# Sums over states after every second unit instead of every fourth, and dt's two matmuls half a unit apart

## The chip, the cores and the metric

One core of one Trainium2 chip runs the whole program in one launch. The time is the device time of one execution in microseconds. The engines are TensorE (PE), VectorE (DVE), ScalarE (ACT), GpSimd (POOL) and SyncE (SP), which issues every DMA here. Each engine takes its own instructions strictly in order; semaphores make one wait for another. PSUM, the memory that PE writes, has eight banks of 128 x 512 float32.

## The reference, cut to what matters

Two layers run one after the other on 8 images of 64 x 64 tokens with 192 channels. The first is a chunked state-space layer with convolutions and an MLP in front of and behind it. In the second, half of the channels go through convolutions and the other half through a selective scan in four directions; that scan is where the change lies:

```python
x_dbl = jnp.einsum('bkdl,kcd->bkcl', xs4, x_proj_w)      # xs4: the four directions, 192 channels
dts, Bs, Cs = ...                                        # 6, 16 and 16 rows of x_dbl
delta = jax.nn.softplus(jnp.einsum('bkrl,kdr->bkdl', dts, dt_proj_w) + dt_proj_b[None, :, :, None])
A = -jnp.exp(A_logs)
def step(h, t):
    u_t, d_t, b_t, c_t = t
    h = jnp.exp(d_t[..., None] * A) * h + (d_t * u_t)[..., None] * b_t[:, :, None, :]
    return (h, jnp.einsum('bkdn,bkn->bkd', h, c_t))      # the sum over the 16 states
```

## The kernel before

**Tiling.** A step is 1024 of an image's 4096 tokens in one pair of directions: 8 steps per image. A step has three tiles of 128 channel rows. A tile has 16 units. A unit is 8 channel rows times 16 states, so 128 partitions by 1024 columns. That gives 384 units per image and 3072 in all. "Place" below is a unit's number in its tile, 0 to 15.

**A unit.** `fetch` (L1432, SP) reads dt from DRAM, repeated for the 16 states, six units ahead. `decay` (L1437, ACT) makes exp(dt A) of it in place, two units at a time. `spread` (L1445, PE) makes dt u for all states by one matmul for each half of the columns, into one of two buffers of two banks each. `weigh` (L1462, DVE) multiplies that with B in place. `scan` (L1469, DVE) runs the recurrence into a tile h. POOL saves the last column as the carry (L1471) and multiplies h with C in place (L1472). `gather` (L1483, PE) sums over the states.

**The sums.** `gather` is called at unit q for the four units q-5 to q-2, in every fourth unit. The constant `k["gather"]` has 32 columns, of which 8 hold something. The four units go to four groups of 32 partitions of one bank, one matmul each, for one half of the columns; half a unit later ACT copies the bank to y (L1488), and the other half of the columns follows in another bank, with its copy another half unit later. Two units on, `store` (L1496) issues four DMAs of 8 x 1024.

**dt.** `prepare` is a generator that makes the next tile's dt and dt u while the current tile's units run. It yields the number of the half unit at which it wants to go on. At the first half of place 0 it issues both dt matmuls (L1390), each into a bank of its own, half a unit later both softplus (L1394, ACT), later the product du = dt u (L1396, POOL), the store of dt (L1399), the split of du into three bf16 terms (L1404 to L1410, ACT and POOL by turns) and their DMAs (L1413, L1421).

**The order.** It is written out by hand; `pin` keeps it. The loop over q issues, for each unit: `fetch`, `weigh`, a new `gather` or `store` where due, and then two halves. Each half goes on with the gather, then with the work beside (`beside.half`), then with `prepare`; the first half ends with `spread(q + 1)` and `scan(q)`, the second, in odd units, with two decays. The work beside is everything else: the layers of the next image and the convolutions, sums and outputs of the one before, as generators that yield a cost at each piece. Each half adds a rate to a credit; the work beside runs until the credit is used up, and `beside.spend` charges the scan's own matmuls to it.

**Banks.** Everything but the spread takes single banks from a ring of four (`cx.one`): dt, the sums and all of the work beside. Who takes a bank waits until the last reader of its former contents is done.

**Buffers.** `np_` is a pool of two buffers for each name unless `bufs` says otherwise: y has two, h seven (`4 + BEHIND + 1` with `BEHIND = 2`).

Of the kernel before, what the change touches and what calls it, by code (L numbers as in the profile page):

```python
# [9 lines left out]
F32 = mybir.dt.float32  # L10
# [28 lines left out]
LC = 1024  # L39
UD = 128 // NS  # L40
UN = 128 // UD
DTS = (64, 96)
# [1257 lines left out]
def selective_scan(cx, us, ys, beside, images, start_image, tail):  # L1300
# [8 lines left out]
    nc, tc, pin, k = cx.nc, cx.tc, cx.pin, cx.k  # L1309
    AHEAD, BEHIND = 6, 2  # L1310
    halves = [slice(q * 512, (q + 1) * 512) for q in range(LC // 512)]
# [10 lines left out]
    def order(ap, g):  # L1322
        return reversed_free(ap) if g == 1 else ap
# [8 lines left out]
    with (  # L1332
# [7 lines left out]
        dAs, dBs, hs, late = {}, {}, {}, []  # L1340
# [36 lines left out]
        def prepare(n):  # L1377

            m, t = tiles[n]
            image, g, s = steps[m]
            rows = rows_of[m][0]
            bias = k["dtb"][:, g, t : t + 1]
            dl, du = (wp.tile([128, LC], F32, tag=v, name=v) for v in ("dl", "du"))
            pss = [cx.one("ps_dt") for here in halves]
            for ps, at, here in zip(pss, DTS, halves):
                took = slice(at, at + 2 * RK)
                pin(nc.tensor.matmul(ps, lhsT=k["dtw"][took, g, t, :], rhs=rows[took, here], start=True, stop=True))  # L1390
            beside.spend(1.2)
            yield 1
            for ps, here in zip(pss, halves):
                pin(nc.scalar.activation(dl[:, here], ps, AF.Softplus, bias=bias))  # L1394
            yield 3
            pin(nc.gpsimd.tensor_mul(du, dl, u_of[m][t]))  # L1396
            yield 6
            dld = dp.tile([128, LC], F32, tag="dld", name="dld")
            pin(nc.sync.dma_start(out=dld, in_=dl))  # L1399
            delta_of[n] = dld  # L1400
            yield 7

            terms = wp.tile([128, 3, LC], BF16, tag="terms", name="terms")
            pin(nc.scalar.copy(terms[:, 0, :], du))  # L1404
            yield 9
            pin(nc.gpsimd.tensor_sub(du, du, terms[:, 0, :]))
            yield 11
            pin(nc.scalar.copy(terms[:, 1, :], du))
            yield 13
            pin(nc.gpsimd.tensor_sub(terms[:, 2, :], du, terms[:, 1, :]))  # L1410
            yield 17
            dud = dp.tile([3, 128, LC], BF16, tag="dud", name="dud")
            pin(nc.sync.dma_start(out=dud.rearrange("s p l -> p s l"), in_=terms))  # L1413
            yield 21

            dus = np_.tile([128, UN // 2, 512], BF16, tag="dus", name="dus")
            for half in range(2):
                for odd in range(2):
                    at = 32 * (2 * odd + half)
                    for v in range(3):  # L1420
                        pin(nc.sync.dma_start(  # L1421
                            out=dus[at + UD * v : at + UD * (v + 1)],
                            in_=dud[v].rearrange("(i odd c) l -> odd c i l", odd=2, c=UD)[odd][:, :, halves[half]],
                        ))
                if half == 0:
                    yield 23
            du_of[n] = dus
# [22 lines left out]
        def of(q):  # L1450

            n, i = units[q]
            m, t = tiles[n]
            image, g, s = steps[m]
            more = s != (L // LC - 1, 0)[g]
            bc = bc_of[m, (i // 8 if t == 2 else t)]
            return *bc, carries[image, g][:, t, i : i + 1], 0 if g == 1 else LC - 1, g, more

        def weigh(q):

            dBs[q] = dBs[q].rearrange("p a b -> p (a b)")
            pin(nc.vector.tensor_mul(dBs[q], dBs[q], of(q)[0]))  # L1462

        def scan(q):

            _, C_, carry, last, g, more = of(q)
            dA, dB = dAs.pop(q), dBs.pop(q)
            h = hs[q] = np_.tile([128, LC], F32, tag="h", name="h", bufs=4 + BEHIND + 1)
            pin(nc.vector.tensor_tensor_scan(order(h, g), order(dA, g), order(dB, g), carry, ALU.mult, ALU.add))  # L1469
            if more:  # L1470
                pin(nc.gpsimd.tensor_copy(carry, h[:, last : last + 1]))  # L1471
            pin(nc.gpsimd.tensor_mul(h, h, C_))  # L1472

        def gather(q):

            n, i = units[q]
            m, t = tiles[n]
            image, g, s = steps[m]
            y = np_.tile([128, LC], F32, tag="y", name="y")
            for here in halves:  # L1480
                ps = cx.one("acc")
                for v in range(4):
                    pin(nc.tensor.matmul(  # L1483
                        ps[32 * v : 32 * (v + 1)], lhsT=k["gather"], rhs=hs[q - 3 + v][:, here], start=True, stop=True
                    ))
                beside.spend(1.6)
                yield
                pin(nc.scalar.copy(y[:, here], ps))  # L1488
            for v in range(4):
                del hs[q - 3 + v]  # L1490
            late.append((ys(image)[g][t][UD * (i - 3) : UD * (i + 1), s * LC : (s + 1) * LC], y))

        def store():
            rows, y = late.pop()
            for v in range(4):
                pin(nc.sync.dma_start(out=rows[UD * v : UD * (v + 1)], in_=y[32 * v : 32 * v + UD]))  # L1496

        for t in range(3):
            load(0, t)
# [4 lines left out]
        for _ in prepare(0):  # L1504
            pass
# [5 lines left out]
        coming, due, following, gathering = None, 0, None, iter(())  # L1511
        for q in range(U + BEHIND):
            n, at = divmod(q, UN)
            if q < U:
                m, t = tiles[n]
# [9 lines left out]
                if t == 2 and m + 1 < len(steps):  # L1525
                    image = steps[m + 1][0]
# [9 lines left out]
                if q + AHEAD < U:  # L1536
                    fetch(q + AHEAD)
                weigh(q)
            if (q - BEHIND) % 4 == 3 and q > BEHIND:
                gathering = gather(q - BEHIND)  # L1540
            if (q - BEHIND) % 4 == 1 and q > BEHIND + 1:
                store()
            if q < U:
                for half in range(2):
                    next(gathering, None)
                    beside.half()
                    if coming is not None and 2 * at + half == due:
                        due = next(coming, 2 * UN)
                    if following is not None and t == 2 and at >= UN - 5:
                        next(following, None)  # L1550
                    if half == 0:
                        if q + 1 < U:
                            spread(q + 1)
                        scan(q)
                    elif q % 2 == 1:
                        for ahead in (q + 2, q + 3):
                            if ahead < U:
                                decay(ahead)
        for _ in gathering:
            pass  # L1560
        store()
        beside.finish()
        tail()
# [155 lines left out]
```

## Time and profile before

| What | us |
|---|---|
| runs | 16338.47, 16344.59, 16351.96 |
| their median | 16344.59 |
| the profiled execution's own time | 16347.41 |
| its span, first to last instruction | 16345.0 |
| mean granted TensorE clock | 0.826 |
| first and last scan begin at | 906.3 and 16096.7 |
| an image in the middle (2728 to 4710; 4711 to 6689) | 1982; 1978 |
| PE, DVE, POOL, ACT busy in the second of these | 1630, 1526, 1365, 1142 |
| the last image (14553 to 16100) | 1547 |

The page has one row for each group of instructions: line, engine, operation, output and inputs, shapes and count, then busy time in us and mean duration in ns, then the engine's idle time just before these instructions and what ended most of it. The views of waits give, for an engine's instruction and the instruction that released it, the sum of the idle time in us, how often it occurred, and the longest. A float32 matmul of the source is two rows of PE. Four matmuls on four groups of the array's columns run at the same time, so a row's mean duration is longer than its share of the busy time.

### The profile page before, as it was taken

Reading aid. Unit: us, or ns where it says so; the run is one execution under the profiler, and the core shown is the slowest. Engines: PE = TensorE matmul, PEld = TensorE weight load, DVE = VectorE, ACT = ScalarE, POOL = GpSimd, SP = SyncE. Lnnn points to the kernel's source line nnn. Section 1 sums busy time; section 2 is a strip of 40 time slices with the busy share of each in tenths; the row PEclk is TensorE's granted clock in tenths of the full one; section 3 lists DMA queues with packets and bytes.
Section 4 is the critical chain, followed back from the end, with each engine's and each line's share of the span. In section 5 each row is a group of like instructions: output and inputs, shape, how many; then the busy total and the mean of one; then the engine's idle time right before and its main releaser. Section 6 shows DMA issues by size and latency. Waiting matters only on the chain. (4 is left out here: it accounts for less than half of the span.)

```text
span 16345.0 us, 208335 instructions
## 1 busy us (share of the span) xinstructions
PE 13293.7 (81%) x69608; PEld 4607.8 (28%) x69608; DVE 12235.6 (75%) x9264; ACT 9072.0 (56%) x13776; POOL 10935.8 (67%) x8070
## 2 busy tenths in 40 slices
PE   8977887789887898778888788887887778878866
PEld 4422322333223322233213332133322333211111
DVE  2168887887778867788677886788867887778894
ACT  3355565555665547655466554664656555654643
POOL 3158766876668766687666865678666776667773
PEclk9987787789787897878978798787988889777776
DMA  3288888788787887878878788887888878788885
GB/s 90 83 208 192 209 204 211 199 202 222 187 218 188 210 216 190 221 185 220 213 194 208 189 216 208 204 207 194 219 200 212 204 202 226 188 228 213 208 214 134
DMA packets 1602566, 3241.15 MB, mean 198 GB/s; under 512 B 390152, under 2 KB 841368, under 8 KB 1601496
## 3 DMA queue, kind: packets, MB, share of 16 engines
q1 hardware_dynamic: 1601496, 3227.83, 78.7%
q8 instruction: 556, 9.11, 0.3%
q14 instruction: 514, 4.21, 0.1%
HBM read 2548.91 MB, written 678.18 MB: 197 GB/s over the span
## 5 line engine op out<-in xcount | busy, mean ns | idle before, releaser
L1472 POOL TENSOR_TENSOR h<-h,bc 128x1024 f32<-128x1024 f32 x3072 | 7238.9, 2357 | 1310.3 <-DVE h L1469 1030.6
L1469 DVE TENSOR_TENSOR_SCAN h<-dA,carry,dB 128x1024 f32<-128x1024 f32 x3072 | 7200.3, 2344 | 581.1 <-ACT dA L1437 253.2
L1462 DVE TENSOR_TENSOR dB<-dB,bc 128x1024 f32<-128x1024 f32 x3072 | 3737.5, 1217 | 1860.1 <-PE dB L1445 1855.4
L1437 ACT ACTIVATE dA<-dA,neg_a 128x1024 f32<-128x1024 f32 x3072 | 3378.0, 1150 | 255.2 <-DMA dA<-dld 237.3
L1483 PE MATMUL acc<-h,gather 128*32 128x512 f32 x12288 | 2235.5, 729 | 289.2 <-POOL h L1472 113.9
L1471 POOL COPY carry<-h 128x1 f32<-128x1 f32 x2304 | 422.5, 183 | 2728.3 <-DVE h L1469 2555.1
L1445 PE MATMUL dB<-dus,spread 24*128 24x512 bf16 x6144 | 1386.8, 439 | 866.9 <-DVE h L1469 799.8
L1488 ACT COPY y<-acc 128x512 f32<-128x512 f32 x1536 | 891.6, 580 | 1811.9 <-issue 1021.1
L886 PE MATMUL ps_c<-p,conv_w 96*96 96x512 f32 x2304 | 1261.3, 673 | 31.3 <-ACT p L906 31.3
L1445 PEld LDWEIGHTS <-spread 24*128 24x128 bf16 x6144 | 308.9, 93 | 3074.6 <-issue 1438.0
L690 PE MATMUL ps_y<-X,M 64*64 64x64 f32 x12288 | 613.7, 274 | 419.9 <-issue 187.4
L339 PE MATMUL ps_cv<-pad,diag 64*64 64x512 f32 x6912 | 847.0, 605 | 15.7 <-ACT y L1488 10.0
L618 ACT ACTIVATE M<-ps_d,ln_dt 128x64 f32<-128x64 f32 x3072 | 671.9, 336 | 292.0 <-PE ps_d L624 217.6
L690 PEld LDWEIGHTS ps_y<-X,M 64*64 64x64 f32 x12288 | 559.9, 184 | 598.8 <-issue 233.3
L1483 PEld LDWEIGHTS acc<-h,gather 128*32 128x32 f32 x12288 | 293.7, 117 | 1227.3 <-issue 555.1
L623 PE MATMUL ps_d<-R,after 128*128 128x384 f32 x1024 | 596.8, 675 | 34.1 <-ACT bc L612 16.1
L612 ACT COPY bc<-ps_t 64x256 f32<-64x256 f32 x256 | 93.7, 366 | 929.8 <-PE ps_t L607 929.5
L886 PEld LDWEIGHTS ps_c<-p,conv_w 96*96 96x96 f32 x2304 | 367.5, 177 | 772.4 <-issue 701.4
L1437 ACT ACT_TABLE_LOAD x445 | 570.9, 1283 | 7.9
L1358 PE MATMUL ps_xp<-u,xp 128*108 128x512 f32 x768 | 467.3, 695 | 97.1 <-DMA u<-u 83.6
L1396 POOL TENSOR_TENSOR du<-dl,u 128x1024 f32<-128x1024 f32 x192 | 452.2, 2355 | 136.6 <-DMA bcd<-rows 82.9
L369 PE MATMUL ps_h<-oa,w1a 128*128 128x256 f32 x1536 | 465.0, 424 | 61.0 <-ACT y L1488 21.0
(245 smaller groups left out, 18086.6 us busy)
## 6 DMA issues: line engine op xcount, KB each, us to landing
dA<-dld SPq DMA_DIRECT2D x3072, 512.0 KB
dud<-terms SPq DMA_DIRECT2D x192, 768.0 KB
dus<-dud SPq DMA_DIRECT2D x2304, 64.0 KB
bc<-bcd SPq DMA_DIRECT2D x256, 512.0 KB
y<-yrows SPq DMA_DIRECT2D x256, 384.0 KB
u<-u SPq DMA_DIRECT2D x192, 512.0 KB
dld<-dl SPq DMA_DIRECT2D x192, 512.0 KB
y<-y SPq DMA_DIRECT2D x3072, 32.0 KB
```

What stands on the lines that cost most here:

```text
L339: pin(nc.tensor.matmul(ps[64 * b : 64 * (b + 1)].rearrange("p (h w) -> p h w", w=WW), lhsT=diag[:, t, :], rhs=pad[64 * i : 64 * (i + 1), b ...
L618: pin(nc.scalar.activation(M[:, d, h, :], ps[:, h * S : (h + 1) * S], AF.Exp, bias=bias))
L623: pin(nc.tensor.matmul(ps, lhsT=k["after"], rhs=flat(R[:, d * NH : (d + 1) * NH, :]), start=True, stop=False))
L690: pin(nc.tensor.matmul(psy[d][here, h * HP : (h + 1) * HP], lhsT=M[here, d, h, :], rhs=X[here, d, h, :], start=True, stop=True,))
L886: pin(nc.tensor.matmul(ps.rearrange("p (h w) -> p h w", w=WW), lhsT=w[:, t, :], rhs=pad[:, dy : dy + RB, dx : dx + WW], start=t == 0, stop ...
L1437: pin(nc.scalar.activation(dAs[q], dAs[q], AF.Exp, scale=k["neg_a"][:, steps[m][1], t, i : i + 1]))
L1445: pin(nc.tensor.matmul(dBs[q][:, half, :], lhsT=k["spread"][at : at + 3 * UD, :], rhs=du_of[n][at : at + 3 * UD, i // 2, :], start=True, s ...
L1462: pin(nc.vector.tensor_mul(dBs[q], dBs[q], of(q)[0]))
L1469: pin(nc.vector.tensor_tensor_scan(order(h, g), order(dA, g), order(dB, g), carry, ALU.mult, ALU.add))
L1472: pin(nc.gpsimd.tensor_mul(h, h, C_))
L1483: pin(nc.tensor.matmul(ps[32 * v : 32 * (v + 1)], lhsT=k["gather"], rhs=hs[q - 3 + v][:, here], start=True, stop=True))
L1488: pin(nc.scalar.copy(y[:, here], ps))
```

## The change

`gather` is called in every second unit, for the two units q-3 and q-2. Both halves of the columns of both units go into one bank: first half to partitions 0 to 63, second half to 64 to 127. One copy moves the bank to y, whose shape is now pair, column: two pairs fill one y. `store` runs at the same place and issues four DMAs as before, one for each half of the columns and each unit of a pair, with rows of 512 instead of 1024 values. h has six buffers instead of seven.

`prepare` issues the first dt matmul in half 0, in half 1 its softplus and the second matmul, in half 2 the second softplus, and goes on with du in half 4 instead of 3. Each of the two is charged 1.0 to the credit, where the pair was charged 1.2.

```diff
-            pss = [cx.one("ps_dt") for here in halves]
-            for ps, at, here in zip(pss, DTS, halves):
+            for later, (at, here) in enumerate(zip(DTS, halves)):
+                ps = cx.one("ps_dt")
                 took = slice(at, at + 2 * RK)
                 pin(nc.tensor.matmul(ps, lhsT=k["dtw"][took, g, t, :], rhs=rows[took, here], start=True, stop=True))
-            beside.spend(1.2)
-            yield 1
-            for ps, here in zip(pss, halves):
+                beside.spend(1.0)
+                yield 1 + later
                 pin(nc.scalar.activation(dl[:, here], ps, AF.Softplus, bias=bias))
-            yield 3
+            yield 4
             pin(nc.gpsimd.tensor_mul(du, dl, u_of[m][t]))
...
-            h = hs[q] = np_.tile([128, LC], F32, tag="h", name="h", bufs=4 + BEHIND + 1)
+            h = hs[q] = np_.tile([128, LC], F32, tag="h", name="h", bufs=2 + BEHIND + 2)
...
-            y = np_.tile([128, LC], F32, tag="y", name="y")
-            for here in halves:
-                ps = cx.one("acc")
-                for v in range(4):
+            pair = i // 2 % 2
+            if pair == 0:
+                y = np_.tile([128, 2, 512], F32, tag="y", name="y")
+                late.append((ys(image)[g][t][UD * (i - 1) : UD * (i + 3), s * LC : (s + 1) * LC], y))
+            y = late[-1][1]
+            ps = cx.one("acc")
+            for half, here in enumerate(halves):
+                for v in range(2):
+                    at = 32 * (2 * half + v)
                     pin(nc.tensor.matmul(
-                        ps[32 * v : 32 * (v + 1)], lhsT=k["gather"], rhs=hs[q - 3 + v][:, here], start=True, stop=True
+                        ps[at : at + 32], lhsT=k["gather"], rhs=hs[q - 1 + v][:, here], start=True, stop=True
                     ))
-                beside.spend(1.6)
-                yield
-                pin(nc.scalar.copy(y[:, here], ps))
-            for v in range(4):
-                del hs[q - 3 + v]
-            late.append((ys(image)[g][t][UD * (i - 3) : UD * (i + 1), s * LC : (s + 1) * LC], y))
+            beside.spend(1.6)
+            yield
+            pin(nc.scalar.copy(y[:, pair, :], ps))
+            for v in range(2):
+                del hs[q - 1 + v]

         def store():
-            rows, y = late.pop()
-            for v in range(4):
-                pin(nc.sync.dma_start(out=rows[UD * v : UD * (v + 1)], in_=y[32 * v : 32 * v + UD]))
+            rows, y = late.pop(0)
+            rows = rows.rearrange("(p v c) l -> v c p l", p=2, v=2)
+            for half, here in enumerate(halves):
+                for v in range(2):
+                    at = 32 * (2 * half + v)
+                    pin(nc.sync.dma_start(out=rows[v][:, :, here], in_=y[at : at + UD]))
...
-            if (q - BEHIND) % 4 == 3 and q > BEHIND:
-                gathering = gather(q - BEHIND)
             if (q - BEHIND) % 4 == 1 and q > BEHIND + 1:
                 store()
+            if (q - BEHIND) % 2 == 1 and q > BEHIND:
+                gathering = gather(q - BEHIND)
```

## The prediction

> **What bounds the kernel now.** I read the page first: its busy times (part 1) and its groups (part 5). Part 4, the chain that ended last, names 1% for its largest entry; the kernel has no single chain that could be followed, so I went on to the waits by engine, then to busy times by stage, then to a piece of timeline.
>
> ```profile
> PE 13293.7 (81%) x69608; PEld 4607.8 (28%) x69608; DVE 12235.6 (75%) x9264; ACT 9072.0 (56%) x13776; POOL 10935.8 (67%) x8070
> ...
> L1469 DVE TENSOR_TENSOR_SCAN h<-dA,carry,dB 128x1024 f32<-128x1024 f32 x3072 | 7200.3, 2344 | 581.1 <-ACT dA L1437 253.2
> L1462 DVE TENSOR_TENSOR dB<-dB,bc 128x1024 f32<-128x1024 f32 x3072 | 3737.5, 1217 | 1860.1 <-PE dB L1445 1855.4
> ...
> L1483 PE MATMUL acc<-h,gather 128*32 128x512 f32 x12288 | 2235.5, 729 | 289.2 <-POOL h L1472 113.9
> ```
>
> A unit needs 2.344 + 1.217 = 3.56 us of DVE, but the 3072 scans, which begin at 906.3 and 16096.7 us, stand (16096.7 - 906.3) / 3071 = 4.95 us apart. No engine is full. The largest single loss on DVE is its wait for dB, the spread matmuls of L1445, which stand in PE's queue behind whatever else PE was given. By stage, in one image:
>
> ```profile
> 4960.00:5560.00 600.00, 455.34 (x3467) 197.07 (x3466) 484.11 (x476) 299.51 (x659) 475.70 (x380) 0.76 0.78 192
> 5930.00:6190.00 260.00, 241.31 (x647) 66.19 (x646) 158.08 (x90) 101.22 (x129) 146.97 (x118) 0.92 0.81 206
> ```
>
> (stretch, its length, busy us of PE, PE's weight loads, DVE, ACT, POOL; then granted clock, DMA share, GB/s.) Beside the chunked layer (L555 to L707) PE, DVE and POOL are each near 80% and wait for one another; beside the convolutions (L886) PE is 93% busy. So PE's order is what sets the pace, and a wait of PE costs time when a spread stands behind it. The waits that the change can reach:
>
> ```profile
> DVE dB L1462 <- PE dB L1445: 1855.4, 762, 98.5
> ...
> PE dB L1445 <- DVE h L1469: 799.8, 375, 24.9
> ...
> PE acc L1483 <- POOL h L1472: 113.9, 95, 4.4
> ...
> PE ps_dt L1390 <- DVE Hn L681: 43.0, 20, 3.3
> ...
> ACT y L1488 <- PE acc L1483: 668.2, 290, 8.5
> ```
>
> The fourth of them, once, on PE and DVE:
>
> ```profile
> 5008.47 1.12 PE L1390 MATMUL ps_dt<-rows,dtw 12*128 12x512 f32 x2
> ...
> 5012.85 1.19 PE L1390 MATMUL ps_dt<-rows,dtw 12*128 12x512 f32 x1 [3.26 <-DVE Hn L681]
> 5012.86 0.60 PE L1445 MATMUL dB<-dus,spread 24*128 24x512 bf16 x1
> ...
> 5015.35 1.23 DVE L1462 TENSOR_TENSOR dB<-dB,bc 128x1024 f32<-128x1024 f32 x1 [1.72 <-PE dB L1445]
> ```
>
> The first dt matmul runs; the second needs a bank that DVE has not read yet (L681), the spread behind it goes late, and DVE loses 1.72 us.
>
> **Part by part.** The sum is made against the profiled execution, 16347.4 us (span 16345.0); the runs' median is 3 us lower.
>
> *The sums' own work: 0.* Before, four matmuls per half of the columns, 1536 such groups at 2235.5 / 1536 = 1.46 us; afterwards four per pair of units, on the same four column groups of the array, 1536 again. Copies: 1536 of 580 ns in both. What changes is the place. The groups stood in two successive halves of every fourth unit, now in the first half of every second; each is followed in both by one spread.
>
> *dt apart: -40.* All idle time of PE ahead of L1390 is 55.9 us (its group), 43.0 of it the wait shown. With half a unit in between, the bank is mostly read by then, and spread(1) no longer stands behind both. Between 0 (the wait moves to the second half) and -56. I take the 41 us which I find ahead of a late dB when I go through the units at which DVE waited for one.
>
> *dt's banks held next to the sums': +15.* PE waits 26.0 us for banks that the softplus (L1394) has to free: its rows name acc, ps_mean, ps_x and ps_p. Before, both are freed before the next sums begin; now the second is held while the sums take theirs. In the built order I counted the claims that come after less than 1.5 us of matmuls (by PE's mean times) since the last read of that bank: in images 1 to 6 dt holds the bank in 47 of them before and 101 after. 26.0 x (101 / 47 - 1) = 30 more at most; half, because about half of PE's waits in front of spreads reach DVE. Between 0 and +30.
>
> *The sums' banks: +30.* PE's waits that end with the copy L1488 add up to 153 us over their rows (22.7 at L445 the largest). By the same count acc holds the bank in 159 tight claims before and 309 after, as its copy now always follows its matmuls by a single half: +144 us at most. Against it acc is the claimer in 185 instead of 262, and acc's own waits for others than POOL are 289.2 - 113.9 = 175 us: -51 at least. Between -51 and +144; a third of the net +93.
>
> *POOL: +30.* A sum over units q-3 and q-2 stands at unit q in PE's order and waits for POOL's product with C (L1472) for unit q-2. Behind it stand the rest of the half and spread(q+1), for which DVE waits. There are twice as many such places now. The new ones fall on units 3, 7, 11, 15 of a tile; the product of unit 5 stands on POOL behind the 2.13 us of L1406. Placing each new sum in the middle of what PE did there, it is late on POOL by 176 us in all, against 249 for the old places by the same rule, which paid 113.9. So 80 more on PE; between 0 and +114, and I take less than half, as the dB after the old waits was late at few places.
>
> *Activation tables: +20.* The row of loads is
>
> ```profile
> L1394 ACT ACT_TABLE_LOAD x192 | 246.3, 1283 | 3.4
> ```
>
> and the built order holds 1355 loads before (the trace has 1355 too) and 1399 after: 20 more ahead of the softplus, since work beside it comes between its halves, and 24 around it. 44 x 1.283 = 56 us of ACT, at 56% busy. What may hide it is ACT's own wait for acc, 668 us; without it the decays (L1437) come late and the scan waits. Between 0 and +56.
>
> The Trainium skill speaks against this part: "ScalarE: Activation LUTs", What ACT_TABLE_LOAD costs, gives some 2.66 us for a switch (load and drain) and asks to batch calls by set. In this trace the next activation starts within 0.02 us of a load's end (5105.80 + 1.28, then 5107.10), so no drain is seen. By the page's figure the 44 loads would take 117 us of ACT and the sum would stand about 20 higher.
>
> *du later: +10.* The product du (L1396) is issued half a unit later. On POOL it still lies between the products of units 1 and 2, but behind one more half of the work beside: (10935.8 - 7238.9 - 452.2 - 409.0 - 408.5 - 422.5) / 6144 = 0.33 us, 192 times 63 us. Behind it wait the cast L1404 (119.7 us already) and, on ACT after it, the decays of units 5 and 6, for which the scan waits; 253.2 us is all that scans lose to decays. Between 0 and +63.
>
> *Stores and buffers: 0.* Four DMAs of 32 KB per four units as before, at the same place on SP, in rows of 2 KB instead of 4: 24,576 more packets at the mean of 0.787 x 16 x 16345 / 1601496 = 0.13 us are 1.2% more of the DMA engines' time at most. SP's queue past them is unchanged, and the copies end half a unit earlier. A y buffer is refilled 4.5 units (22 us) after its store is issued, 6.5 before; by the semaphores the stores land 5 us after issue in the middle and 14 us at most. h has one buffer fewer, but a scan now reuses a buffer summed three units earlier; scans wait for no sum today. If that cover failed, the refill would stall ACT by up to 8 us three times (the stores later than the place of the new refill). Pacing: dt is charged 2.0 instead of 1.2, so 154 units of credit in all move work beside to a later place; each image still ends with none left over. 0 to +30.
>
> Sum: -40 + 15 + 30 + 30 + 20 + 10 = +65, so 16345 + 65 = 16410 us. All low ends together give -107, all high ends +437. They are not met together: half the width of each term (28, 15, 98, 57, 28, 32), added in squares, is 125 us.
>
> **The rivals.** (1) *Nothing to measure*: the gains of the first term and the costs meet; a kernel in which three engines wait for one another in turn gives most moved waits to another. 16345 us. For it: each single term is under 0.4%; against: the order of all work beside shifts, and the stalls repeat in each image alike (1975 us each), so a shift counts six times over. 0.2% (33 us) is about what a measurement can tell.
>
> (2) *Faster, because the pair of dt is what makes a tile's start late.* DVE's waits for dB at a tile's first three units are 209, 196 and 282 us, counted over the trace, against (1855 - 687) / 13 = 90 at the others: 417 us too much. dt's 323.9 / 192 = 1.69 us in one go precede the second of them. If a quarter of the excess goes with the pair, -104, and the sums no longer in two halves running bring as much as POOL costs, 16240 us. It decides from the point where this saving passes the 105 us of my costs. Against: the excess lies in six or so tiles of an image, some 10 us each, where one stage beside gives way to the next.
>
> (3) *PE tied to POOL twice as often costs whole*: +114 for POOL's waits and +30 for the chain of du, 16410 + 84 + 20 = 16514 us. For it: POOL is the engine whose lag changes most, with du's three products of 2.1 to 2.4 us; against: the 95 old waits are short, 1.2 us each.
>
> That the change does not do what it says is out: in the built order the four matmuls stand after every second unit and the dt matmuls on either side of spread(1).
>
> **How the numbers follow.** Slower by a little (16380 to 16470): 0.33. Rival 3 and beyond: 0.12. Rival 1: 0.22. Rival 2 and better: 0.33. Predicted 16410. Slower 0.45, same 0.22, faster 0.33. The range reaches from rival 2 to a little past rival 3: 16240 to 16530; the likeliest case alone, 16380 to 16470.
>
> **What would show it.** L1390's idle time under 25 us; waits of the sums for POOL's h near 190 us; PE's waits for the copies of y above 200 us; ACT_TABLE_LOAD x1399 in all, x212 ahead of the softplus; DVE's wait for dB between 1850 and 1980 us. The prediction is wrong if that wait falls by 100 us, or if another row (the chunked layer's L665, L681, L690) moves by as much.

## The result: slower by 1.5%, and the profile after

The changed kernel takes 16577.57 us (median; 16564.49 to 16642.94) beside 16341.53 us of the kernel before on the same chip: a ratio of 1.0153, 95% interval 1.0125 to 1.0181, or +236 us. The direction was forecast, the size was not: 16410 was predicted, and 16530 was the top of the range. The profiled execution took 16564.49 us, its span 16562.7.

The busy times and groups of the changed kernel (its lines from L1392 on lie 1 lower than before as far as the scan, and up to 6 higher behind it):

```profile
PE 13679.1 (83%) x69608; PEld 4689.4 (28%) x69608; DVE 12212.9 (74%) x9264; ACT 9173.5 (55%) x13820; POOL 10938.1 (66%) x8070
...
L1468 DVE TENSOR_TENSOR_SCAN h<-dA,carry,dB 128x1024 f32<-128x1024 f32 x3072 | 7197.0, 2343 | 642.5 <-ACT dA L1436 344.3
L1461 DVE TENSOR_TENSOR dB<-dB,bc 128x1024 f32<-128x1024 f32 x3072 | 3734.5, 1216 | 1941.8 <-PE dB L1444 1912.5
...
L1487 PE MATMUL acc<-h,gather 128*32 128x512 f32 x12288 | 2460.5, 746 | 490.1 <-POOL h L1471 220.5
...
L1390 PE MATMUL ps_dt<-rows,dtw 12*128 12x512 f32 x768 | 492.7, 797 | 97.5 <-ACT dl L1393 31.7
```

The row of dt before, which stands on the same line:

```profile
L1390 PE MATMUL ps_dt<-rows,dtw 12*128 12x512 f32 x768 | 323.9, 788 | 55.9 <-DVE Hn L681 43.0 <-ACT h L823 2.9 <-ACT za L1232 2.7
```

Every row that the change touches on PE has become dearer: the sums with their idle time went from 2524.7 to 2950.6 us, dt from 379.8 to 590.2. That invites the reading "PE now waits for POOL at the head of its queue, twice as often", and it was the first theory below. But a row on PE is not the time. DVE does the same work as before (12235.6 and 12212.9 us), so the 217.7 us that the span grew, and 22.7 more, are DVE's idle time. The waits of DVE, before

```profile
DVE Hm L665 <- PE ps_s L659: 276.2, 183, 13.8
DVE h L1469 <- ACT dA L1437: 253.2, 48, 23.9
DVE Hn L681 <- POOL Hn L667: 243.1, 164, 7.4
...
DVE va L1011 <- ACT ps_var L1007: 165.3, 47, 9.8
```

and after (us in total, times, longest):

```profile
DVE dB L1461 <- PE dB L1444: 1912.5, 746, 96.1
DVE Hm L665 <- PE ps_s L659: 357.7, 183, 10.2
DVE h L1468 <- ACT dA L1436: 344.3, 87, 31.3
...
DVE Hn L681 <- POOL Hn L667: 198.9, 130, 8.3
DVE va L1011 <- ACT ps_var L1007: 198.2, 58, 9.8
```

The wait for dB, where a delay of the sums was to show, grew by 57 us. The chunked layer's own wait (L665) grew by 82, the wait for decays by 91, the normalisation's (L1011, `va`) by 33; Hn's fell by 44. The loss is spread over waits of lines that the diff does not touch. By stage in one image (the third; stretches between the scans of units 32, 144, 224, 288 and 352, that is, beside the chunked layer, the MLP, the convolutions, and the outputs and next inputs), first before, then after:

```profile
4855.00:5471.00 616.00, 466.95 (x3772) 201.81 (x3771) 509.56 (x480) 329.46 (x709) 502.84 (x418) 0.77 0.78 193
5471.00:5837.00 366.00, 324.93 (x1544) 138.89 (x1538) 309.25 (x221) 230.55 (x305) 255.18 (x145) 0.94 0.91 227
5837.00:6200.00 363.00, 316.51 (x906) 90.26 (x906) 227.95 (x133) 150.86 (x192) 210.26 (x170) 0.89 0.79 204
6200.00:6529.00 329.00, 293.62 (x1038) 68.76 (x1040) 257.07 (x185) 246.26 (x293) 210.20 (x153) 0.79 0.77 190
```

```profile
4845.00:5480.00 635.00, 483.57 (x3782) 201.60 (x3782) 507.47 (x481) 338.00 (x714) 504.66 (x420) 0.76 0.76 187
5480.00:5856.00 376.00, 329.39 (x1544) 141.19 (x1544) 308.33 (x222) 234.81 (x309) 254.70 (x145) 0.94 0.87 217
5856.00:6193.00 337.00, 313.33 (x912) 89.87 (x912) 227.77 (x133) 150.79 (x189) 205.45 (x165) 0.93 0.85 221
6193.00:6547.00 354.00, 307.51 (x1037) 70.25 (x1038) 256.66 (x184) 251.66 (x299) 214.31 (x157) 0.76 0.73 177
```

(The columns are those of the prediction's stages.) The second column is the length: +19 and +10 us beside the chunked layer and the MLP, then -26 and +25, as if a stall had changed its stage.

### The profile page after: what moved, and what is told of

Same layout as the page of the kernel before. It is cut to its first block, busy times and chain, and to the rows that moved or that the text cites. A ratio compares the mean times of both kernels' runs of the same rounds, so it can differ in the third digit from the quotient of the medians.

```text
span 16562.7 us, 209230 instructions
## 1 busy us (share of the span) xinstructions
PE 13679.1 (83%) x69608; PEld 4689.4 (28%) x69608; DVE 12212.9 (74%) x9264; ACT 9173.5 (55%) x13820; POOL 10938.1 (66%) x8070
## 5 line engine op out<-in xcount | busy, mean ns | idle before, releaser
L1461 DVE TENSOR_TENSOR dB<-dB,bc 128x1024 f32<-128x1024 f32 x3072 | 3734.5, 1216 | 1941.8 <-PE dB L1444 1912.5
L1487 PE MATMUL acc<-h,gather 128*32 128x512 f32 x12288 | 2460.5, 746 | 490.1 <-POOL h L1471 220.5
L1444 PE MATMUL dB<-dus,spread 24*128 24x512 bf16 x6144 | 1422.5, 439 | 663.6 <-DVE h L1468 395.6
L690 PE MATMUL ps_y<-X,M 64*64 64x64 f32 x12288 | 568.3, 259 | 423.3 <-DVE Hn L681 168.2
L690 PEld LDWEIGHTS ps_y<-X,M 64*64 64x64 f32 x12288 | 511.6, 169 | 622.1 <-issue 202.9
L1390 PE MATMUL ps_dt<-rows,dtw 12*128 12x512 f32 x768 | 492.7, 797 | 97.5 <-ACT dl L1393 31.7
```

The lines of the kernel that those rows point to most:

```text
L690: pin(nc.tensor.matmul(psy[d][here, h * HP : (h + 1) * HP], lhsT=M[here, d, h, :], rhs=X[here, d, h, :], start=True, stop=True,))
L1444: pin(nc.tensor.matmul(dBs[q][:, half, :], lhsT=k["spread"][at : at + 3 * UD, :], rhs=du_of[n][at : at + 3 * UD, i // 2, :], start=True, s ...
L1487: pin(nc.tensor.matmul(ps[at : at + 32], lhsT=k["gather"], rhs=hs[q - 1 + v][:, here], start=True, stop=True))
```

## The experiments

Eighteen kernels in five groups, in the order in which they ran. In the expectations, theory S says that the sums at the head of PE's queue wait for POOL; theory D that dt's two matmuls, no longer together, cost their lost concurrency; theory M that only the planner's choices matter; theory N that the kernel before stands at a narrow optimum of them. Kernels of a group share the runs of the kernel before (medians 16351.6, 16353.3, 16350.4, 16347.0, 16362.8 us by group).

| group | kernel | us | ratio, 95% interval |
|---|---|---|---|
| 1 | sums alone, dt as before | 16568.45 | 1.0133 (1.0114 to 1.0151) |
| 1 | change, sums one unit later | 16377.81 | 1.002 (1.0005 to 1.0035) |
| 1 | change, dt's pair kept | 16578.74 | 1.0141 (1.0125 to 1.0157) |
| 1 | layout alone, four units as before | 16326.89 | 0.9984 (0.9974 to 0.9995) |
| 2 | one unit later, dt as before | 16568.47 | 1.0132 (1.0118 to 1.0146) |
| 2 | change, decays on even units | 16529.63 | 1.0111 (1.0097 to 1.0125) |
| 2 | change, sums two units later | 16629.8 | 1.0168 (1.0152 to 1.0185) |
| 2 | layout alone, one unit later | 16363.21 | 1.0006 (0.9995 to 1.0018) |
| 3 | before, charges of the change | 16632.46 | 1.0174 (1.0158 to 1.0189) |
| 3 | change, charges of before | 16553.31 | 1.0124 (1.0109 to 1.0139) |
| 3 | one unit later, dt together, other charges | 16414.02 | 1.0041 (1.0027 to 1.0056) |
| 4 | sums on odd units, charges on even | 16720.72 | 1.024 (1.022 to 1.026) |
| 4 | sums on even units, charges on odd | 16679.68 | 1.0204 (1.0183 to 1.0226) |
| 4 | before, charge 1.7 for 1.6 | 16660.09 | 1.019 (1.0169 to 1.0211) |
| 4 | layout and dt apart, charges of before | 16302.02 | 0.9976 (0.9966 to 0.9987) |
| 5 | change, charge 1.5 | 16607.59 | 1.0171 (1.0137 to 1.0204) |
| 5 | change, charge 1.7 | 16521.09 | 1.0097 (1.0078 to 1.0116) |
| 5 | before, charge 1.5 | 16588.95 | 1.0142 (1.0123 to 1.016) |

### Group 1: which part of the change

**Sums alone.** The changed kernel with `prepare` as before.

> The changed kernel with dt as before: both dt matmuls together in half 0, both softplus in half 1, du in half 3, charged 1.2. Theory S (the sums, met twice as often, wait for POOL's product and for banks at the head of PE's queue; PE's time on them, busy and idle, rose from 2524 to 2950 us) and theory D (the two dt matmuls ran at the same time on two row groups and no longer do; 1.69 us a tile became 2.57, 169 us in all): this keeps S and undoes D, so about 16342 + 140 = 16480 us, with L1390 back at about 324 us busy and the sums' idle time still near 490. Rival R (softplus in two places, the 44 table loads and the later du cost the time): at or under 16380, with the sums' idle time as in the changed kernel all the same. Rival N (nothing of dt matters): 16575.

**dt's pair kept.** The changed kernel with both dt matmuls together, but du late and charged 2.0, as the change has it:

```diff
+            pss = [cx.one("ps_dt") for here in halves]
...
-                beside.spend(1.0)
+            beside.spend(2.0)
+            for later, (ps, here) in enumerate(zip(pss, halves)):
                 yield 1 + later
```

> The changed kernel with both dt matmuls together in half 0 again, but softplus still in halves 1 and 2, du in half 4, charged 2.0 as changed. Theory D: L1390 goes back to about 324 us busy and the time is within 30 us of that of the run with dt wholly as before (about 16480). Rival R (softplus apart, table loads, du later): the time stays near 16575, though L1390 is back.

**Layout alone.** The kernel before with the new layout of bank, y and stores; both pairs are summed one after the other in every fourth unit:

```diff
-            for here in halves:
+            for pair in range(2):
                 ps = cx.one("acc")
...
-                        ps[32 * v : 32 * (v + 1)], lhsT=k["gather"], rhs=hs[q - 3 + v][:, here], start=True, stop=True
+                            ps[at : at + 32], lhsT=k["gather"], rhs=hs[q - 3 + 2 * pair + v][:, here], start=True, stop=True
```

> The kernel before with the new layout of the sums alone: two units and both halves of the columns in one bank, y and stores as changed, but both pairs one after the other in every fourth unit, in two successive halves as before; h has seven buffers, dt as before. Theory S: it is how often PE meets POOL that costs, not the layout: 16342 within 30 us, the sums' busy time near 2236 and idle time near 289. Rival L (the layout, copies or the stores of 2 KB rows cost): 16420 or more.

**Sums one unit later.** The changed kernel with a lag of three units, which puts the sums on even units:

```diff
-    AHEAD, BEHIND = 6, 2
+    AHEAD, BEHIND = 6, 3
...
+            else:
+                for _ in gathering:
+                    pass
```

(The last lines issue the sums that are due after the last unit.)

> The changed kernel with BEHIND 3 instead of 2: each sum stands one unit later in PE's queue, h has seven buffers as before. Theory S: POOL's product is done when PE comes to the sum, so the sums' idle time that ends with POOL falls from 220 us to under 40, and the time falls by 80 to 160 us from the changed kernel's, to 16420 to 16500. Theory D: it does not touch dt, so at least the 100 us or so of dt remain. Rival B (banks and copies, not POOL, are what the sums cost): POOL's wait goes, but the idle time moves to others and the time stays within 40 us of 16575.

Sums alone took 16568.45 us, the kept pair 16578.74: dt has no part in the loss that could be measured, though keeping the pair brought L1390 back from 492.7 to 308.0 us. Layout alone took 16326.89, a little less than before. A lag of three brought 200 of 236 us back, and the wait for POOL's h left the row of the sums (2059.8 us busy, 178.2 idle):

```profile
L1487 PE MATMUL acc<-h,gather 128*32 128x512 f32 x12288 | 2059.8, 745 | 178.2 <-DVE yo L697 76.5
```

All of this fits theory S. But a lag of three had changed two more things: the parity of the units on which the sums stand, and the halves in which they are charged.

### Group 2: the wait for POOL goes, the loss stays

**Sums two units later.** A lag of four: odd units again, and POOL four units ahead.

```diff
-    AHEAD, BEHIND = 6, 2
+    AHEAD, BEHIND = 6, 4
...
-            h = hs[q] = np_.tile([128, LC], F32, tag="h", name="h", bufs=2 + BEHIND + 2)
+            h = hs[q] = np_.tile([128, LC], F32, tag="h", name="h", bufs=2 + BEHIND + 1)
...
```

(The last lines are those of the lag of three.)

> The changed kernel with the sums four units behind instead of two (seven h buffers, one spare), so that they fall on odd units as in the changed kernel, y copy right in front of the decays. Theory S: as far as the run with a lag of three, 16380 within 30; the row of the sums shows no wait for POOL's h worth telling (under 20 us) and some 2060 busy. Rival P: back near the changed kernel, 16550 within 40, since the copies precede the decays again.

**Decays on even units.** The changed kernel with the decays moved away from the copies:

```diff
-        for q in range(3):
+        for q in range(2):
             decay(q)
...
-                    elif q % 2 == 1:
+                    elif q % 2 == 0:
                         for ahead in (q + 2, q + 3):
```

> The changed kernel, with the decays of two units issued after the even units instead of the odd ones, so that they no longer stand right behind a y copy in ScalarE's queue; the sums stay two units behind. The run with the sums one unit later (16377.8) changed this too, as a lag of three makes the sums fall on even units. Theory S (PE is in order, and the sums at the head of its queue wait for POOL's h times C of two units before; now at every second unit): the parity has nothing to do with it, 16560 within 30, and the sums' idle time ahead of them stays near 490 us with over 180 us ended by POOL's h. Rival P (a y copy right in front of the decays makes the decays late, so scans, so PE): most of the loss goes, 16400 within 40, and DVE's waits for dA (344 us) fall to under 260.

**One unit later, dt as before.** The lag of three with `prepare` as before (both matmuls together, charged 1.2).

> The changed kernel with the sums three units behind and dt's two matmuls back together (both softplus in half 2), so only the sums' layout and frequency differ from the kernel before, at a lag of three. It asks what dt's separation costs once PE no longer waits for POOL. Theory S with dt hidden: 16370 within 20, no different from the 16378 with dt apart. Rival D (with POOL's wait gone, dt's lost concurrency, 2.57 against 1.69 us a tile, shows on PE): 192 x 0.88 = 169 us less at most, 16210; half of it 16290. L1390 back near 320 us.

**Layout alone, one unit later.** Layout alone with `BEHIND = 3`.

> The kernel before with the new layout of sums, y and stores, both pairs every fourth unit, and the sums three units behind instead of two; h keeps seven buffers, which leaves none spare. With a lag of two this layout took 16326.9. Theory S: the wait for POOL's h ahead of the sums (48.8 us by its row) goes, and with it something of the split groups: 16290 within 25. Rival: nothing is left to gain once three of four sums have no wait, 16327 within 15. Rival B: the lost spare buffer makes scans wait for the sums, over 16370, and L1468's idle time shows a wait for the sums.

With a lag of four the kernel took 16629.8 us, no less than the changed kernel (the intervals of the two ratios overlap), and this is its row of the sums:

```profile
L1487 PE MATMUL acc<-h,gather 128*32 128x512 f32 x12288 | 2107.8, 764 | 263.8 <-ACT h L823 70.8 <-DVE yo L697 55.0 <-ACT po L462 29.7
```

POOL's h has nearly vanished from it (7.5 us in the waits), 352.7 us of PE's busy and 226.3 of its idle time are saved, and nothing is gained. In all but 209 of 6144 halves it issues the same amount of work beside as the changed kernel. So theory S, as it was put, fails: taking the wait for POOL away did not bring the time back.

One thing clouds this. The granted clock of the lag of four was 0.801 to 0.806 in its four executions, that of the changed kernel 0.815 to 0.823. In the 62 executions of the kernel before that the groups share, a straight line through clock and time gives some 75 us more for each 0.01 less. By that estimate some 140 us of this kernel's time go with its clock, so a gain from the missing wait may lie hidden beneath it. No run separates the two.

With the decays on even units, away from the copies, 48 us came back; but ScalarE then loaded its tables 357 times more often than before (14133 against 13776 instructions; 357 x 1.283 = 458 us), so what the copies alone cost is not shown. And dt together with a lag of three took 16568.47, 191 us more than dt apart with that lag: a sign opposite to theory D's. The two also differ in what dt charges, 1.2 in one half or 1.0 in each of two. That pointed at the planner.

### Group 3: the charges alone

`beside.spend` issues nothing. It lowers the credit, and so decides in which half the next piece of the other stages is issued. The change moved it along with the sums: 1.6 in the first half of every second unit, where 1.6 in two halves of every fourth stood. Counted in the built programs, 3609 of 6144 halves then issue another amount of work beside. The two kernels here separate the charges from the instructions.

**Before, with the charges of the change:**

```diff
-            beside.spend(1.2)
+            beside.spend(1.0)
             yield 1
+            beside.spend(1.0)
...
-                beside.spend(1.6)
                 yield
...
                     next(gathering, None)
+                    if q % 2 == 1 and q > BEHIND and half == 0:
+                        beside.spend(1.6)
                     beside.half()
```

> The kernel before with all its own instructions, in its own halves (four units' sums in two halves of every fourth unit, dt's two matmuls together), but with the changed kernel's charges: 1.6 in the first half of every second unit instead of 1.6 in both halves of every fourth, and 1.0 in each of two halves for dt instead of 1.2 in one. Only where the planner puts the work of the other stages changes; a log of the planner's choices is the same, half by half, as that of the changed kernel. Theory M (the charges moved with the sums, and so shifted where the pieces of the other stages fall among the scans; that shift is the loss): 16560 within 40. Rival S (the sums themselves, twice as often at the head of PE's queue): 16345 within 30.

**The change, with the charges of before:** the reverse (1.6 in both halves of units with q % 4 == 1; 1.2 and 0 for dt).

> The reverse: the changed kernel with all its own instructions, sums every second unit and dt's two matmuls half a unit apart, but with the charges of the kernel before (1.6 in both halves of every fourth unit, 1.2 in the first half of dt), so that the planner puts every piece of the other stages into the half it had before. Theory M: 16345 within 40. Rival S: 16560 within 40. If both this and the run before lie in the middle, the two share the loss, or it is that plan and sums no longer fit together.

**One unit later, dt together, charged 1.0 in each of two halves** instead of 1.2 in one.

> The run with sums three units behind and dt's two matmuls together (16568.5) against the one with dt apart (16377.8) differ by 190 us; dt's charges differ as well (1.2 in one half against 1.0 in each of two). This is the former with the latter's charges. Theory M: 16378 within 30. Rival D (dt's matmuls apart are themselves worth 190 us at that lag): 16568 within 30.

The kernel before, all of its own instructions where they were, lost 282 us from the charges alone, more than the whole change costs. Its waits on DVE for L659 and for the decays are those of the changed kernel, not its own, and the one for dB is longer than in either:

```profile
DVE dB L1463 <- PE dB L1446: 2013.6, 716, 98.2
DVE Hm L665 <- PE ps_s L659: 349.4, 189, 9.9
DVE h L1470 <- ACT dA L1438: 338.1, 63, 31.5
```

The reverse did not take the loss away, though: the changed kernel with the old plan, the same in every half, took 16553.31, still +203. Its wait for dB, where a delay of the sums was to show, is 169 us longer than before:

```profile
DVE dB L1461 <- PE dB L1444: 2024.1, 793, 99.4
DVE Hm L665 <- PE ps_s L659: 335.2, 169, 13.1
DVE h L1468 <- ACT dA L1436: 250.7, 64, 24.7
```

In this kernel DVE's idle time, taken from the begin of one scan to that of the next (mean of the second to sixth image), is 55 us an image longer than before behind units 3, 7, 11 and 15 of a tile, where the sums are new, and 27 shorter at all other units together. Layout and dt apart with the same plan cost nothing (group 4), so what is left to explain the 203 is the new place of the sums, with du's later half and the one buffer of h less. Each half of the change alone thus costs about as much as the two together: 282 us the charges, 203 the instructions, 236 both. And the third run shows 154 of the 191 us between dt together and dt apart to be a matter of charges (16568.47 to 16414.02). DVE's idle time in one image by stretch, in us, the mean of the second to sixth image, added up over the traces:

| units | before | change | before, charges of the change | change, charges of before |
|---|---|---|---|---|
| 0 to 31 | 31.3 | 28.7 | 34.6 | 32.6 |
| 32 to 143, chunked layer | 104.2 | 127.5 | 121.1 | 102.6 |
| 144 to 223, MLP | 58.9 | 70.9 | 76.1 | 70.1 |
| 224 to 287, convolutions | 127.8 | 110.2 | 110.1 | 131.7 |
| 288 to 351, outputs and inputs | 74.2 | 93.2 | 97.3 | 88.9 |
| 352 to 383 | 50.9 | 54.1 | 56.9 | 49.2 |

The first two columns of numbers differ by 37 us an image. Beside the chunked layer and the convolutions the numbers go with the plan (columns 2 and 3 alike, 1 and 4 alike); beside the MLP and the outputs every pairing but the first has 11 to 23 us more.

### Group 4: crossing sums and charges, and a small push

**Sums on odd units, charges on even:** the changed kernel with `spend(1.6)` in the first half of even units.

> The changed kernel's instructions, sums on odd units and two units behind, with the charges of the run with sums one unit later: 1.6 in the first half of every even unit. With sums and charges both on odd units it took 16577.6, both on even units 16377.8. Theory M (only where the pieces of the other stages fall matters): 16380 within 40. Rival O (the odd units matter for the sums' own matmuls and copies, which stand in front of the decays in ScalarE's queue): 16560 within 40. Rival F (sums and charges must fall together): slower than both, over 16600.

**Sums on even units, charges on odd:** the lag of three with the changed kernel's charges.

> The reverse: sums three units behind and on even units, with the charges on odd units, as in the changed kernel. Theory M: 16570 within 40. Rival O: 16380 within 40. Rival F: over 16600.

**Before, charge 1.7.** One number:

```diff
-                beside.spend(1.6)
+                beside.spend(1.7)
```

> The kernel before with nothing changed but the amount that a half's sums are charged: 1.7 instead of 1.6. No instruction of its own changes its half; the pieces of the other stages slip by a few halves against the scans. Theory N (the kernel before stands on a narrow optimum of the plan, and any slip costs 100 to 250 us): 16450 to 16600. Rival: a small slip costs nothing, and the changed plan is bad for a reason of its own: 16350 within 40.

**Layout and dt apart, charges of before.** Layout alone, and dt's matmuls on either side of the half; the plan is that of the kernel before, half by half:

```diff
-            beside.spend(1.2)
-            yield 1
-            for ps, here in zip(pss, halves):
+                beside.spend((1.2, 0.0)[later])
+                if later == 0:
+                    yield 1
```

> The kernel before with the new layout of sums, y and stores (16326.9) and dt's two matmuls half a unit apart, with dt charged 1.2 in the first half as before, so that the plan is the same half by half. Theory H (dt's matmuls, 2.57 instead of 1.69 us a tile, hide in PE's idle time): 16327 within 25. Rival D (they don't): 192 x 0.88 = 169 us more at most, 16500. Rival G (the gain that the prediction gave to it, a shorter hold-up on PE at each tile's start): 16290.

Both crossings are the slowest of all: 16720.72 and 16679.68, that is 143 and 302 us more than the same instructions with charges in their own halves. With group 3 (+282, and -24 where the changed kernel was given the old plan) three of four crossings lose. Charges that stand away from their matmuls were mostly the worse, then; but in the changed kernel (16577.57) they stand with them, and it is slow all the same.

The push asks how much weight a single number has. 1.7 instead of 1.6, with no instruction of the scan's own in another half, gave 3442 of 6144 halves another amount of work beside and cost the kernel before 313 us. Its waits and its stages (same units of the same image as above):

```profile
DVE dB L1462 <- PE dB L1445: 2018.5, 713, 100.9
DVE Hm L665 <- PE ps_s L659: 329.3, 183, 6.9
DVE h L1469 <- ACT dA L1437: 318.2, 91, 23.4
```

```profile
4887.00:5511.00 624.00, 491.98 (x3740) 210.52 (x3739) 506.90 (x475) 331.95 (x712) 504.22 (x419) 0.74 0.80 193
5511.00:5899.00 388.00, 332.88 (x1564) 142.08 (x1560) 310.07 (x225) 236.86 (x312) 254.27 (x146) 0.90 0.83 209
5899.00:6246.00 347.00, 308.60 (x933) 90.43 (x930) 228.07 (x134) 148.33 (x188) 208.00 (x168) 0.92 0.84 214
6246.00:6599.00 353.00, 313.94 (x1017) 71.97 (x1017) 257.30 (x184) 247.69 (x295) 212.09 (x155) 0.72 0.74 178
```

In these views it looks much like the changed kernel, without any of its change: L665 up by 53 us, decays by 65, dB by 163; the chunked layer, the MLP and the outputs longer than before (+8, +22, +24), the convolutions shorter (-16). By unit it does not: behind odd units, where the changed kernel's sums stand, DVE's idle time rose by 49 us an image in the changed kernel and fell by 9 here.

With the plan held still, layout and dt apart took 16302.02 us, the fastest of all and faster than both kernels (0.9976, 0.9966 to 0.9987). Whether dt apart gives any of that is not shown: layout alone has 0.9984 (0.9974 to 0.9995), and the intervals overlap. Its rows:

```profile
L1485 PE MATMUL acc<-h,gather 128*32 128x512 f32 x12288 | 2054.2, 741 | 188.5 <-POOL h L1472 54.7 <-ACT h L823 28.0 <-DVE gT L787 18.7
...
L1390 PE MATMUL ps_dt<-rows,dtw 12*128 12x512 f32 x768 | 462.1, 783 | 17.6 <-ACT za L1232 4.0 <-DVE o L1249 3.9 <-ACT u L1069 3.1
```

dt is 138 us dearer on PE than before, which does not show in the time, and its idle time is down to 17.6 us, which is what the prediction expected of the change.

### Group 5: is the changed kernel one draw out of many?

**The change with 1.5 and with 1.7, and before with 1.5**, each by the one number.

> The changed kernel with a unit's sums charged 1.5 instead of 1.6 and nothing else; the stages beside slip by a few halves. Theory N (the changed kernel's plan is one of a spread of plans, as the kernel before with 1.7, 16660, is): anywhere from 16380 to 16680, and this and the run with 1.7 more than 60 apart. Rival O (sums on every second, odd unit cost 200 us whatever the plan; three other plans of them gave 16553 to 16579): 16570 within 30, both.

> The changed kernel with a unit's sums charged 1.7. As for 1.5: theory N 16380 to 16680 and more than 60 from that run, rival O 16570 within 30.

> The kernel before with the sums of a half charged 1.5 instead of 1.6. With 1.7 it took 16660. Theory N (the kernel before stands at a narrow optimum): 16500 to 16700. Rival W (only a slower plan hurts, since with 1.7 the stages beside end late in each image): 16350 within 40.

The changed kernel took 16607.59 and 16521.09, 87 us apart, the better with the charge that hurt the kernel before most; before with 1.5 took 16588.95, +226. So the kernel before loses 226 and 313 us on either side of its own charge: in that one number it stands at a narrow optimum, and a push of it costs about as much as the change. The clock does not account for this: it was 0.005 to 0.015 lower in the three kernels slowed by charges alone, which by the estimate of group 2 is 40 to 115 us of their 226 to 313. Not every other plan is bad: layout alone a unit later differs from before in 3870 halves and took 16363.21, the lag of three in 3775 and took 16377.81.

What stays open: whether the +236 us of the change is such a loss by the plan, or whether sums in every second, odd unit cost some 200 us whatever the plan. Nine kernels with them lie between 16521 and 16721, and none reaches 16350; that rival stands. Nor was it shown which piece of which stage meets which scan.

## Why the prediction was wrong, step by step

**Two steps failed, and how they share the loss stays open.** The first is the clause on pacing, under "Stores and buffers: 0": it counted dt's higher charge, 154 units of credit "in all move work beside to a later place", and gave it 0 to +30 us. The charges of the sums were left out, though they move with the sums in the diff. Measured, the charges alone cost the kernel before 282 us, and 0.1 more or less of one charge 313 and 226.

The second is the price of the sums' new place: 0 for their own work, since "each is followed in both by one spread", and +30 each for banks and for POOL. In the order of the kernel before, the second group of a unit has two halves of work beside between it and the next spread; every new group has one. With the plan held, the changed instructions cost 203 us, and DVE's wait for dB grew by 169; that the shorter distance is the reason is not shown. The sum added its terms as if each kept its price beside the others: 282 and 203 came to 236 together. Rival 1 had named the mechanism ("the order of all work beside shifts, and the stalls repeat in each image alike") and taken it as an argument against no change, without a price.

- *The sums' own work, 0.* Right as the price of the matmuls alone: in the new layout with the old frequency the row is 2055.5 us. In the changed kernel it rose to 2460.5 with nearly the same mean (746 against 742 ns), so the matmuls of a group ran less at the same time; with a lag of four, where the rise is mostly gone, the time was no better.
- *dt apart, -40.* The mechanism is there when the plan stays (L1390's idle 17.6 us), but in the changed kernel its idle rose to 97.5, and PE's work on it by 169 us, which the step had not seen. In time: ratios of 0.9976 with it and 0.9984 without, some 13 us, with overlapping intervals, so nothing shown.
- *dt's banks, +15, and the sums' banks, +30.* PE's waits for the softplus rose from 26.0 to 57.3 us, the 30 of the upper end. Its waits for the copies were to pass 200 us and fell from 153 to 21, so there the count of tight claims in the built order did not carry over. What either is worth in time was not separated.
- *POOL, +30.* 80 more were worked out, 107 came (113.9 to 220.5). A good working of the wait; that it costs time was not shown, as the kernel with 7.5 us of it is no faster. Rival 3, built on this wait, had the nearest time, 16514; as far as the runs go, by luck.
- *Activation tables, +20.* The counts came out exactly (13820 - 13776 = 44 more, 212 ahead of the softplus). That ScalarE hides them is made likely by the run with 357 more than before, which was no slower than the change.
- *du later, +10.* Not separated. *Stores, buffers, 0.* Right for stores and layout: layout alone lost nothing.
- The dB wait of 1912.5 lies inside 1850 to 1980, and L665 moved by 82 us where 100 was to be the alarm. The loss was spread under every threshold.

Giving the range only 120 us above the centre was too little: the kernels run here lie between 16302 and 16721, and that spread, not the sum of the terms, was the measure of uncertainty.

## What to carry to other kernels

Where other work is woven in by a budget, an edit that moves or resizes a charge can change the whole order, and that may cost more than all waits near the edit. Run the old kernel once with a charge a few per cent off before pricing anything; if it loses as much as the edit, the edit itself has not been measured. Then hold the plan still and change the instructions part by part: here layout and dt apart gained 45 us that way, while the sums in every second unit still lost 203, so a bad plan was not the only cost.

## What the runs showed of the hardware

Two matmuls with a contraction of 12 rows, at partitions 64 and 96, run at the same time when issued together: 323.9 / 192 = 1.69 us a tile, against 492.7 / 192 = 2.57 us when a half lies between them. The Trainium skill, "TensorE: Matmul & The Clock Gate", section "Why this matters for your kernels", says the same of small contractions at partitions that are multiples of 32. The change gave that up; keeping the pair brought no time back (16578.74).

The Trainium skill, "Trainium Kernel Development and Optimization", section "Performance Expectations", calls matmul busy time a bad metric for how close a kernel is to its roofline, as matmuls are pipelined. Here PE's busy time does not order the kernels either: 13305.2 us at 16302.02, 13383.9 at 16588.95 (before with 1.5), 13679.1 at 16577.57. Nor does the granted clock across kernels: 0.816 in the fastest, 0.821 in the changed kernel. Among the executions of one kernel a lower clock goes with a longer time (group 2).
